# Pacing the gathers of a four-layer graph network in GpSimd's queue, and letting the tails run four stages in three slots

## The chip, the cores and the metric

The kernel runs on one core of a Trainium2 chip. The metric is the time of one execution on the device in microseconds (us). A core has five engines that work side by side, each through its own queue and in order: TensorE (PE, with its weight loads as PEld), VectorE (DVE), ScalarE (ACT), GpSimd (POOL) and SyncE (SP). [...]

## The reference, cut to what matters

Eight feature matrices of 2048 nodes by 128 numbers go through four layers on one sparse graph (each of the 2048 x 2048 entries of `adj` is set with probability 1/128, so a node has some 16 neighbours). Layers 0 and 1 are graph attention transformers:

```
scores = einsum('bnhd,bmhd->bhnm', Q, K) / sqrt(16); masked by adj; softmax
x = layer_norm(h + attn_out @ Wo + bo)
x = layer_norm(x + relu(x @ W1 + b1) @ W2 + b2)
```

Layers 2 and 3 are GAT layers:

```
h = x @ W;  e = leaky_relu(s_i + s_j), masked by adj;  att = softmax(e)
x = layer_norm(einsum('bij,bjd->bid', att, h) + x)
```

A node needs the rows of its neighbours only. A layer can't start on a node before the last layer has finished all of that node's neighbours.

## The kernel before, in words

**Tiles and lists.** The nodes are sorted by degree and cut into 16 tiles of 128, one node per partition. `CAPS` gives the list length of each tile, 30 for the first down to 11 for the last, 277 neighbour slots in all. At the start the kernel counts, sorts and lists (about 180 us).

**Tables and gathers.** Each layer l has a table in DRAM with one row per node: for all eight matrices keys and values together (2048 numbers, layers 0 and 1) or the projected features and two factors (1040 numbers, layers 2 and 3). For one slot of a tile's list, `gather` (L320) is one indirect DMA issued by GpSimd: 128 rows, one per partition, into one of six `kv` buffers. There are 1108 gathers.

**Chunks.** A layer's work is cut into chunks: two slots of one tile in the attention layers, four in the GAT layers. `every` is the list of all chunks in order. An attention chunk runs DVE at L606 (keys times query), L609 (sums over a head) and L620 (weights times values), ACT at L615 (exponentials) and PE at L630 (adds the slots up in PSUM). A GAT chunk runs small DVE steps at L745 to L751, then L757 (weights times features for six of the matrices) beside L762 on ACT (the other two matrices, two scalings per slot), then L766 on DVE (adds half of the slots to the other half) and L772 on PE.

**Tails.** When a tile's last chunk is done, L455 to L462 and L643 or L649 make its normalised output `o`, and two tails, one per half of the eight matrices, carry it on: transposes (L329), products, norms and the projection for the next layer. A tail is a Python generator. It is cut by `yield` into stages, and each stage issues a few instructions. A norm (`normed`) squares on ACT (L471), raises to the power -0.5 on GpSimd (`rs`, L476, "the power" below; 192 of them) and, two yields later, scales on ACT (L480). When both halves are done, GpSimd scatters the tile's rows into the next layer's table (`put_rows`, L494) and `put[l + 1]` goes up by one. In layer 3 each half is multiplied by the gain (L807), offset (L808) and scattered to the output by GpSimd (L810). The tile `n` that a norm writes has two buffers.

**The order.** The order on each engine is that of the Python code. The loop in `layers` goes over the chunks; `now[0]` is the chunk in turn, `now[1]` the first one not yet fetched. In each pass it calls `fetch` once at the top, and three times `slot`, with the parts of chunks between:

```
def slot():
    advance(threads)
    advance(tails)
    fetch()
```

`advance` runs every generator in its list by one stage. `fetch` issues all gathers of as many chunks as it may: at most three chunks (four in the GAT layers) beyond the one in turn, and only once the table holds what a chunk needs. A GAT layer, and layer 1, begins with seven or more early chunks of tiles 0 and 1 whose lists are sorted so that they need only the first 13, 14 or 15 tiles (`EARLY`, `ORDER`); everything else needs all 16. While the next chunk can't be fetched, the loop runs slots alone.

So at the turn into a GAT layer the last tails of the layer before and the early chunks of the new layer are interleaved in the queues of PE and ACT by the slots.

Of the kernel before, what the change touches and what calls it, by code (L numbers as in the profile page):

```python
# [19 lines left out]
NT = N // P  # L20
# [9 lines left out]
CHUNK = 4 * NB * (D + 2)  # L30
# [6 lines left out]
BASE, MANY, FOLD = 28, 16, 2  # L37
# [45 lines left out]
def sparse_path(ctx: ExitStack, tc: tile.TileContext, ins: dict, out: bass.AP, flag: bass.AP):  # L83
# [60 lines left out]
    def buffer():  # L144
        turn[0] += 1
        return bufs[turn[0] % KVB]
# [4 lines left out]
    lists = const.tile([P, sum(CAPS)], I32, name="lists")  # L151
    lmask = const.tile([P, sum(CAPS)], F32, name="lmask")
    first = [sum(CAPS[:t]) for t in range(NT)]

    sorted_lists = const.tile([P, BASE + CAPS[1]], I32, name="sorted_lists")
# [146 lines left out]
    def width(l):  # L302
        return NB * (2 * D if l < 2 else D + 2)
# [15 lines left out]
    def gather(l, index, dst):  # L319
        nc.gpsimd.indirect_dma_start(  # L320
            out=dst, out_offset=None, in_=tables[l][:, :],
            in_offset=bass.IndirectOffsetOnAxis(ap=index, axis=0),
            bounds_check=N - (l < 2), oob_is_err=False,
        )
# [137 lines left out]
        nc.vector.reciprocal(sums, sums)  # L462
        return sums

    def normed(z, dst):

        yield

        ss = small.tile([P, 4], F32, tag="ss", name="ss", bufs=3)
        for i in range(4):  # L470
            nc.scalar.activation(  # L471
                dst[:, i, :], z[:, i, :], AF.Square, bias=eps, scale=D**-0.5,
                accum_out=ss[:, i : i + 1],
            )
        rs = small.tile([P, 4], F32, tag="rs", name="rs", bufs=3)
        nc.gpsimd.tensor_tensor(rs, ss, half, op=ALU.pow)  # L476
        yield
        yield
        for i in range(4):
            nc.scalar.mul(dst[:, i, :], z[:, i, :], rs[:, i : i + 1])  # L480
        yield
# [154 lines left out]
    def sums(l, t, box):  # L636
        box["r"] = reciprocal_sums(l, t, box["w"], NB * (NH if l < 2 else 1), box.get("folded"))
# [353 lines left out]
    def verdict():  # L991
        ok = small.tile([P, 5], F32, tag="ok", name="ok", bufs=1)
        every = score.rearrange("p a t b -> p (a t b)")
        nc.vector.tensor_reduce(ok[:, 3:4], every, axis=AX.X, op=ALU.max)
        nc.vector.tensor_reduce(ok[:, 4:5], every, axis=AX.X, op=ALU.min)
        nc.vector.tensor_single_scalar(ok[:, 3:4], ok[:, 3:4], SCORE_MAX, op=ALU.is_le)
        nc.vector.tensor_single_scalar(ok[:, 4:5], ok[:, 4:5], -SCORE_MAX, op=ALU.is_ge)
        nc.vector.tensor_mul(ok[:, 3:4], ok[:, 3:4], ok[:, 4:5])
        nc.vector.tensor_reduce(ok[:, 0:1], dmin.rearrange("p a b -> p (a b)"), axis=AX.X, op=ALU.min)
        nc.vector.tensor_reduce(ok[:, 1:2], dmax.rearrange("p a b -> p (a b)"), axis=AX.X, op=ALU.max)  # L1000
        nc.vector.tensor_reduce(ok[:, 2:3], over.rearrange("p a b -> p (a b)"), axis=AX.X, op=ALU.max)
        nc.vector.tensor_single_scalar(ok[:, 0:1], ok[:, 0:1], SUM_MIN, op=ALU.is_ge)
        nc.vector.tensor_single_scalar(ok[:, 1:2], ok[:, 1:2], SUM_MAX, op=ALU.is_le)
        nc.vector.tensor_single_scalar(ok[:, 2:3], ok[:, 2:3], 0.0, op=ALU.is_le)
        nc.vector.tensor_mul(ok[:, 0:1], ok[:, 0:1], ok[:, 1:2])
        nc.vector.tensor_mul(ok[:, 0:1], ok[:, 0:1], ok[:, 2:3])
        nc.vector.tensor_mul(ok[:, 0:1], ok[:, 0:1], ok[:, 3:4])
        pk = misc()
        nc.tensor.matmul(pk[:1, :1], ok[:, 0:1], onesc, start=True, stop=True)
        bad = small.tile([1, 1], I32, tag="bad", name="bad", bufs=1)  # L1010
        nc.vector.tensor_scalar(bad, pk[:1, :1], -1.0, float(P), op0=ALU.mult, op1=ALU.add)
        nc.sync.dma_start(flag, bad)
# [3 lines left out]
    tails = []  # L1016

    put = [NT, 0, 0, 0]
    every = []
    blocks = [[{} for _ in range(NT)] for _ in range(4)]  # L1020
    for l in range(4):
        per = 2 if l < 2 else 4
        for t, k, ns, folded in pieces(l, per):
            c = dict(l=l, t=t, k=k, ns=ns, folded=folded, box=blocks[l][t])
            c["last"] = not folded and k + ns == (CAPS[t] if t > 0 else BASE)
            c["run"] = (attention_chunk if l < 2 else gat_chunk)(l, c)
            every.append(c)
    now = [0, 0]

    def advance(group):  # L1030
        for g in list(group):
            if next(g, 0) == 0:
                group.remove(g)

    def fetch():

        while now[1] < len(every):
            c = every[now[1]]
            l, t, k, ns = c["l"], c["t"], c["k"], c["ns"]

            if now[1] - now[0] > (4 if now[1] >= KVB and every[now[1] - KVB]["l"] > 1 else 3):
                return
            resorted = l > 0 and t < 2 and not c["folded"]
            need = NT - max([b for end, b in EARLY[t] if k + ns <= end] + [0] if resorted else [0])
            if put[l] < need:
                return
            c["buf"] = buffer()[:, : ns * width(l)].rearrange("p (s c) -> p s c", s=ns)
            for i in range(ns):
                at = t * BASE if resorted else first[t]
                index = (sorted_lists if resorted else lists)[:, at + k + i : at + k + i + 1]  # L1050
                gather(l, index, c["buf"][:, i])
            now[1] += 1

    def slot():
        advance(threads)
        advance(tails)
        fetch()

    def drain():
        while threads or tails:  # L1060
            advance(threads)
            advance(tails)

    def later(n, make):
        for _ in range(n):
            yield
        yield from make()

    def tail(l, t, box):
        for _ in range(2 if l < 2 else 3):  # L1070
            yield
        outputs(l, t, box)
        part = attention_tail if l < 2 else gat_tail
        tails.append(later(1, lambda: part(l, t, box, 0)))
        tails.append(later(4, lambda: part(l, t, box, 4)))
        yield

    def state(l, t):
        if t >= NT:
            l, t = l + 1, t - NT  # L1080
        if l == 0:
            threads.append(fetch_state(t, blocks[l][t]))
        elif l < 4:
            blocks[l][t].update(x=load_state(t), ready=True)

    def begin(c):
        if c["l"] < 2:
            threads.append(attention_begin(c["l"], c["t"], c["box"]))

    def chunk(i):  # L1090
        return every[i] if 0 <= i < len(every) else dict(l=None, k=None, last=False, folded=False)

    def go(c, times=1):

        for _ in range(times if c["l"] is not None else 0):
            next(c["run"], None)

    def layers():
        threads.append(find_lists(0))
        state(0, 0)  # L1100
        drain()
        fetch()
        begin(every[0])
        drain()
        threads.append(find_lists(1))
        for i in range(len(every) + 2):
            now[0] = i
            fetch()
            c2, c1, c, n1, n2 = (chunk(i + j) for j in range(-2, 3))
            if c["k"] == 0:  # L1110
                l, t = c["l"], c["t"]
                if l == 0:
                    if t + 2 < NT:
                        threads.append(find_lists(t + 2))
                    if t == 0:
                        state(0, 1)
                        threads.append(later(12, lambda: state(0, 2) or iter(())))
                        threads.append(later(12, clear_late))
                    if t in (2, 6):
                        threads.append(order_lists(t // 4))  # L1120
                while l < 2 and "asked" not in c["box"]:
                    slot()
            while i < len(every) and now[1] <= i:
                slot()
            if n2["k"] == 0:
                begin(n2)

            if c2["l"] in (0, 1):  # L1130
                go(c2)
                if c2["last"]:
                    threads.append(tail(c2["l"], c2["t"], c2["box"]))
            if n1["l"] in (2, 3) and n1["folded"]:
                go(n1)
            if c1["l"] in (2, 3) and c1["last"]:
                sums(c1["l"], c1["t"], c1["box"])
            go(c)
            slot()
            go(c)  # L1140
            slot()
            if c1["l"] in (0, 1) and c1["last"]:
                sums(c1["l"], c1["t"], c1["box"])
            go(c1, 2)
            if c1["l"] in (2, 3) and c1["last"]:
                threads.append(tail(c1["l"], c1["t"], c1["box"]))
            slot()
        verdict()
        drain()

    with tc.manual_schedule():
        start()
        layers()
# [525 lines left out]
```

## Time and profile before

| what | value |
|---|---|
| time, median of 4 runs | 3420.86 us (3419.24 to 3422.98) |
| profiled execution, its own time | 3414.06 us |
| its span | 3412.3 us |
| busy: PE, DVE, ACT, POOL | 2747.1, 3062.8, 1427.3, 2216.7 us |
| gathers L320 from `lists` / `sorted_lists` | 955 at 1479 ns, 153 at 1313 ns |
| powers L476 | 192 at 1558 ns |
| DMA | 986.52 MB, mean 289 GB/s |

The page cuts the span into 40 slices of 85 us. Layer 0 begins at about 180 us, layer 1 at about 1200, layer 2 at about 2230 and layer 3 at about 2790. In a row of waits the columns are: engine, line waited at, what ended the wait, total us, times, longest us. In a timeline the columns are: start, duration, engine, line, operation, operands, count, and in brackets the idle time before it with what ended it. Idle time "issue" is time in which the engine waited for nothing that the profile shows.

### The profile page before, as it was taken

Reading aid. Unit: us, or ns where it says so; the run is one execution under the profiler, and the core shown is the slowest. Engines: PE = TensorE matmul, PEld = TensorE weight load, DVE = VectorE, ACT = ScalarE, POOL = GpSimd, SP = SyncE. Lnnn points to the kernel's source line nnn. Section 1 sums busy time; section 2 is a strip of 40 time slices with the busy share of each in tenths; the row PEclk is TensorE's granted clock in tenths of the full one; section 3 lists DMA queues with packets and bytes.
Section 4 is the critical chain, followed back from the end, with each engine's and each line's share of the span. In section 5 each row is a group of like instructions: output and inputs, shape, how many; then the busy total and the mean of one; then the engine's idle time right before and its main releaser. Section 6 shows DMA issues by size and latency. Waiting matters only on the chain.

```text
span 3412.3 us, 34694 instructions
## 1 busy us (share of the span) xinstructions
PE 2747.1 (81%) x10618; PEld 1585.8 (46%) x10618; DVE 3062.8 (90%) x2727; ACT 1427.3 (42%) x4972; POOL 2216.7 (65%) x1501
## 2 busy tenths in 40 slices
PE   5657888888989997788888989985888985667775
PEld 4423455545555553455545555652445543223332
DVE  7789999999999999999999999975888875788886
ACT  5711333334444442233333444443655653444444
POOL 0056788688657654465676766646788765688874
PEclk9878989989999999899999999988999997889888
DMA  8587787888888777687887887757999986889883
GB/s 332 190 319 276 292 293 278 312 298 289 307 316 297 290 264 292 226 328 292 307 321 293 299 307 291 274 196 258 338 340 348 345 308 237 282 296 318 297 291 129
DMA packets 200881, 986.52 MB, mean 289 GB/s; under 512 B 32174, under 2 KB 33968, under 8 KB 128692
## 3 DMA queue, kind: packets, MB, share of 16 engines
q0 software_dynamic: 175280, 890.45, 72.0%
q1 hardware_dynamic: 20502, 75.52, 5.9%
q10 hardware_dynamic: 4904, 18.24, 1.4%
q8 instruction: 87, 1.43, 0.2%
q14 instruction: 108, 0.88, 0.1%
HBM read 937.16 MB, written 91.55 MB: 301 GB/s over the span
## 4 chain that ended last, share of the span: by engine, by line
DVE 33%; PE 24%; issue 18%; DMA 10%; POOL 6%; ACT 3%; POOLq 0%; DVEq 0%; ACTq 0%
DVE kv L620 11%; DVE kv L606 11%; PE acc L630 8%; PE acc L772 6%; DMA kv<-table,lists 5%; POOL kv L320 5%; DMA kv<-table,sorted_lists 2%; DVE sc L609 2%; DVE kv L757 2%; DVE kv L766 2%; PE m L712 2%; PE m L691 1%; PE m L329 1%; POOL rs L476 1%; DVE sums L455 1%
## 5 line engine op out<-in xcount | busy, mean ns | idle before, releaser
L320 POOL DMA_INDIRECT kv<-table,lists x955 | 1412.0, 1479 | 359.1 <-issue 210.6
L630 PE MATMUL acc<-kv,ident 128*128 128x512 f32 x2200 | 1112.3, 636 | 223.8 <-DVE kv L620 223.3
L772 PE MATMUL acc<-kv,ident 128*128 128x512 f32 x1184 | 613.4, 667 | 203.3 <-DVE kv L766 156.4
L630 PEld LDWEIGHTS acc<-kv,ident 128*128 128x128 f32 x2200 | 414.7, 202 | 659.8 <-issue 371.2
L606 DVE TENSOR_TENSOR kv<-kv,q 128x2048 f32<-128x2048 f32 (+1 forms) x282 | 629.2, 2231 | 19.1 <-DMA kv<-table,lists 10.0
L609 DVE TENSOR_REDUCE sc<-kv 128x128 f32<-128x2048 f32 (+1 forms) x284 | 634.0, 2232 | 9.2
L620 DVE TENSOR_TENSOR kv<-kv,w 128x2048 f32<-128x2048 f32 (+1 forms) x284 | 631.4, 2223 | 5.8 <-ACT w L615 5.8
L476 POOL TENSOR_TENSOR rs<-ss,half 128x4 f32<-128x4 f32 x192 | 299.1, 1558 | 413.1 <-ACT n L471 411.4
L471 ACT ACTIVATE n<-m,eps 128x128 f32<-128x128 f32 x768 | 271.3, 366 | 567.8 <-PE m L712 215.7
L772 PEld LDWEIGHTS acc<-kv,ident 128*128 128x128 f32 x1184 | 241.4, 214 | 505.8 <-issue 296.6
L757 DVE TENSOR_TENSOR kv<-kv,pair 128x3072 f32<-128x3072 f32 (+1 forms) x150 | 466.2, 3108 | 1.0
L766 DVE TENSOR_TENSOR kv<-kv 128x2048 f32<-128x2048 f32 (+1 forms) x150 | 296.1, 1974 | 143.1 <-ACT kv L762 143.1
L762 ACT ACTIVATE kv<-kv,ws 128x128 f32<-128x128 f32 x1108 | 339.2, 405 | 146.9 <-DVE ws L751 119.7
L480 ACT ACTIVATE n<-m,rs 128x128 f32<-128x128 f32 x768 | 218.9, 369 | 364.8 <-POOL rs L476 364.3
L615 ACT ACTIVATE w<-sc,lmask 128x64 f32<-128x64 f32 x554 | 164.9, 351 | 457.5 <-DVE sc L609 457.2
L320 POOL DMA_INDIRECT kv<-table,sorted_lists x153 | 200.8, 1313 | 113.9 <-PE acc L630 43.7
L329 PE MATMUL m<-ident,n 128*128 128x128 f32 x640 | 106.2, 287 | 81.5 <-ACT n L480 81.4
L494 POOL DMA_INDIRECT table<-rows,perm x57 | 101.1, 1774 | 106.8 <-ACT rows L518 27.7
L471 ACT ACTIVATION_READ_ACCUMULATOR n<-m,eps 128x1 f32 x768 | 157.3, 205 | 0.0
L712 PE MATMUL m<-w_L_w,hT 128*128 128x128 f32 x1024 | 156.2, 275 | 0.0
L329 PEld LDWEIGHTS m<-ident,n 128*128 128x128 f32 x640 | 81.1, 145 | 138.0 <-ACT n L480 87.2
L712 PEld LDWEIGHTS m<-w_L_w,hT 128*128 128x128 f32 x1024 | 134.9, 192 | 0.0
(234 smaller groups left out, 3252.7 us busy)
## 6 DMA issues: line engine op xcount, KB each, us to landing
kept<-xT SPq DMA_DIRECT2D x48, 512.0 KB, 7.1
xT<-kept SPq DMA_DIRECT2D x48, 512.0 KB, 6.7
kv<-in_adj_dram SPq DMA_DIRECT2D x16, 1024.0 KB, 6.3
table<-kv ACTq DMA_DIRECT2D x16, 1024.0 KB, 4.9
kv<-table,lists POOLq DMA_INDIRECT x955, 7.1
kv<-in_x_nodes_dram SPq DMA_DIRECT2D x16, 512.0 KB, 6.9
kv<-table,sorted_lists POOLq DMA_INDIRECT x153, 6.4
found<-cand POOLq DMA_DIRECT2D x16, 64.0 KB, 3.3
```

The source lines that it names most:

```text
L320: nc.gpsimd.indirect_dma_start(out=dst, out_offset=None, in_=tables[l][:, :], in_offset=bass.IndirectOffsetOnAxis(ap=index, axis=0), bound ...
L471: nc.scalar.activation(dst[:, i, :], z[:, i, :], AF.Square, bias=eps, scale=D**-0.5, accum_out=ss[:, i : i + 1],)
L476: nc.gpsimd.tensor_tensor(rs, ss, half, op=ALU.pow)
L606: nc.vector.tensor_mul(kk, kk, q[:, None].to_broadcast([P, ns, NB, D]))
L609: nc.vector.tensor_reduce(sc[:, :ns].rearrange("p s (b h) -> p (s b) h", h=NH), kk.rearrange("p s b (h j) -> p (s b) h j", h=NH), axis=AX. ...
L620: nc.vector.tensor_mul(vv, vv, w[:, k : k + ns, :].rearrange("p s (b h) -> p (s b) h", h=NH)[:, :, None, :] .to_broadcast([P, ns * NB, HD, ...
L630: nc.tensor.matmul(acc[:, j, :], merge if c["folded"] else ident, kv[:, i, 4 * j : 4 * j + 4, D:], start=k + i == 0, stop=c["last"] and i ...
L712: nc.tensor.matmul(y[:, j, :], hT[:, f, j, :], wt["2"][:, f, :], start=False, stop=f == 1, skip_group_check=True,)
L757: nc.vector.tensor_mul(hv[:, :, :nv, :], hv[:, :, :nv, :], wc[:, :, :nv, None].to_broadcast([P, ns, nv, D]))
L762: nc.scalar.mul(hv[:, i, b, :], hv[:, i, b, :], ws[:, i, b - nv : b - nv + 1])
L766: nc.vector.tensor_add(hv[:, : ns - left], hv[:, : ns - left], hv[:, left:ns])
L772: nc.tensor.matmul(acc[:, j, :], merge if c["folded"] else ident, hv[:, i, 4 * j : 4 * j + 4, :], start=k + i == 0, stop=c["last"] and i = ...
```

## The change

`fetch` issues gathers one at a time and remembers in `now[2]` how far a chunk has come. If the chunk after the one in turn is already fetched, one call issues at most one gather (layers 0 and 1) or two (layers 2 and 3); else as many as it may, as before. The call at the top of a pass is made only if the next chunk isn't fetched yet. Within a slot `fetch` comes after the tails' stages, so what the tails issue on GpSimd in that slot stands ahead of the slot's gathers.

`hurry` holds while the chunk in turn is of the last tile of layer 2, or of a GAT layer whose table is not full yet. Then the tails advance once more in every third slot. `normed` gets a parameter for its two yields, which no caller sets.

```diff
-    def normed(z, dst):
+    def normed(z, dst, wait=2):
...
-        yield
-        yield
+        for _ in range(wait):
+            yield
...
-    now = [0, 0]
+    now = [0, 0, 0]
+    beat = [0]
...
     def fetch():
 
-        while now[1] < len(every):
+        for _ in range((1 if every[min(now[1], len(every) - 1)]["l"] < 2 else 2)
+                       if now[1] > now[0] + 1 else 2 * CHUNK):
+            if now[1] == len(every):
+                return
             c = every[now[1]]
...
-            c["buf"] = buffer()[:, : ns * width(l)].rearrange("p (s c) -> p s c", s=ns)
-            for i in range(ns):
-                at = t * BASE if resorted else first[t]
-                index = (sorted_lists if resorted else lists)[:, at + k + i : at + k + i + 1]
-                gather(l, index, c["buf"][:, i])
-            now[1] += 1
+            i = now[2]
+            if i == 0:
+                c["buf"] = buffer()[:, : ns * width(l)].rearrange("p (s c) -> p s c", s=ns)
+            at = t * BASE if resorted else first[t]
+            index = (sorted_lists if resorted else lists)[:, at + k + i : at + k + i + 1]
+            gather(l, index, c["buf"][:, i])
+            now[1:] = (now[1] + 1, 0) if i + 1 == ns else (now[1], i + 1)
+
+    def hurry():
+
+        c = every[min(now[0], len(every) - 1)]
+        return c["l"] == 2 and c["t"] == NT - 1 or c["l"] > 1 and put[c["l"]] < NT
 
     def slot():
         advance(threads)
         advance(tails)
         fetch()
+        beat[0] += 1
+        if beat[0] % 3 == 0 and hurry():
+            advance(tails)
...
             now[0] = i
-            fetch()
+            if now[1] <= i + 1:
+                fetch()
```

## The prediction

> **What bounds the kernel now.** I read the page first, then busy time by stage, then who waits for whom, then the timeline.
>
> ```profile
> DVE  7789999999999999999999999975888875788886
> POOL 0056788688657654465676766646788765688874
> DMA  8587787888888777687887887757999986889883
> ```
>
> DVE's row is nines through the attention layers (slices 3 to 26) and drops where the GAT layers begin. The same by stage (columns: busy us of PE, PE's loads, DVE, ACT, POOL, then PE clock, DMA share, GB/s):
>
> ```profile
> 200.00:2230.00 2030.00, 1761.20 (x7206) 1041.60 (x7207) 1995.04 (x1191) 751.69 (x2611) 1350.71 (x787) 0.94 0.80 294
> 2230.00:2340.00 110.00, 74.87 (x335) 46.26 (x334) 54.89 (x53) 49.55 (x184) 49.08 (x44) 0.83 0.53 188
> 2340.00:2780.00 440.00, 369.45 (x1397) 207.17 (x1395) 375.61 (x401) 239.00 (x943) 348.74 (x281) 0.94 0.94 340
> 2780.00:2880.00 100.00, 64.76 (x260) 38.61 (x261) 55.63 (x54) 46.00 (x183) 51.57 (x44) 0.81 0.65 228
> 2880.00:3345.00 465.00, 325.29 (x792) 145.96 (x791) 392.67 (x436) 205.67 (x777) 365.09 (x287) 0.87 0.88 300
> ```
>
> Attention: DVE 1995 of 2030 us. The two turns into a GAT layer: DVE half idle. Inside the GAT layers POOL is the full one, although the page says 65%: its instructions follow each other with a fixed gap of about 0.30 us. Gaps counted up to 0.31 us each, from the timeline, POOL is taken for 349 + 77 = 426 of 440 us in layer 2 and 365 + 80 = 445 of 465 in layer 3. What DVE waits for from 2230 on:
>
> ```profile
> DVE kv L766 <- ACT kv L762: 143.1, 52, 9.5
> DVE kv L745 <- DMA kv<-table,lists: 45.9, 2, 33.3
> DVE kv L745 <- DMA kv<-table,sorted_lists: 27.5, 9, 10.6
> ```
>
> L762 is late because ACT stands at L480 for the power (`ACT n L480 <- POOL rs L476`, 364 us in all). One such wait:
>
> ```profile
> 2284.58 0.99 POOL L320 DMA_INDIRECT kv<-table,sorted_lists  x1 [0.30 <-issue]
> 2285.87 0.99 POOL L320 DMA_INDIRECT kv<-table,sorted_lists  x1 [0.30 <-issue]
> 2286.89 1.05 POOL L476 TENSOR_TENSOR rs<-ss,half 128x4 f32<-128x4 f32 x1
> 2287.97 1.14 ACT L480 ACTIVATE n<-m,rs 128x128 f32<-128x128 f32 x4 [7.71 <-POOL rs L476]
> ```
>
> The squares ended at 2277.5; the power ran at 2286.9, behind eight gathers.
>
> **What the Trainium skill says.** "Perfetto Trace Analysis", What "DMA-bound" means: an issuing engine whose track is solid DMA slices is itself the limit; the trace agrees, as above. Same page, DMA Instruction — SWDGE: the slice is descriptor generation, not movement; here 1.0 to 3 us against 7.1 us to landing. "SBUF — State Buffer", Who interferes with whom: a DVE instruction with two SBUF inputs blocks a GpSimd one that reads SBUF; of 80 GAT gathers longer than 1.8 us, 76 begin while L766 (two SBUF inputs) runs. "DMA: Bandwidth & Descriptors", Two DMAs through the same engine are not ordered: a dependent DMA waits for the semaphore; after each L494 the next gather stands 3 to 5 us.
>
> **The change, part by part.** No instruction is added or removed: 1108 gathers, 192 powers, 57 scatters into tables in both. `wait=2` is the old pair of yields: nothing. By the order of the instructions in each queue, DVE's and SP's are the same in both programs, PE's and ACT's differ at the two turns alone, and POOL's differs all through.
>
> *Powers among gathers, layers 2 and 3.* 55 powers now stand after two gathers of a chunk, not after all. A power is 2 x (1.03 + 0.30) = 2.7 us earlier in the queue, and DVE's usual 5.6 us stop at L766 once per tile could shrink to 3. But the same 4.2 us-plus of gathers per chunk still pass through POOL, which has only 14 us of other idle time in layer 2 and 20 in layer 3. DVE gains until L745 waits for gathers in place of L766 for the power. Layer 2: **-4** (0 to -14).
>
> *Outputs, layer 3.* L810 goes out in the slot before the chunk's gathers, four gathers (5 us) earlier. The next tile's squares wait for that store, since `n` has two buffers: 57 us of ACT waits, longest 10.7. With POOL's two gathers between L810 and the next power, the idle 5.9 + 1.7 + 5.6 us at 2949 to 2970 mostly goes: -10; elsewhere -3. **-13** (0 to -20, POOL's spare time).
>
> *Turn 1 to 2* (2230 to 2340). The last table scatter is at 2318.5; DVE stands 33.3 us for the gather behind it. In the new order the second half's first power of tile 15 is ahead of the eight gathers: -9. `hurry` takes four tail stages per three slots, so one chunk's eight scales (2.4 us) and eight matmuls (3.6) fewer are ahead of the tail: -6. Against it, the gathers of the fifth early chunk (2250 to 2257 before) stand behind the first half's power, whose squares end at 2271: DVE gets that chunk at about 2279, +5. **-10** (+3 to -18).
>
> *Turn 2 to 3* (2780 to 2880). Scatters at 2809.2, 2833.1, 2859.4. Each waits for the landing of gathers of the same table, and gathers then for it. The first now has 12 gathers ahead of it, not 16; the fourth chunk moves behind it. Down the new queue, with 1.3 us a gather or power, some 6.5 us from the last gather to landing and 4 us after a scatter: the first gathers start at 2775.7 as before, the twelfth is out at about 2792.5 and landed at 2799, scatter one; from 2803 eight gathers and two powers, out at 2816, landed at 2823, scatter two; from 2827 eight gathers and the last tile's powers, out at 2840; then its scaling, transpose and copies, 8 us as before (2849.8 to 2858.9 with a chunk's scales between): scatter three at 2848. **-11** (0 to -18). What follows a turn is POOL-full and starts earlier, so it isn't lost later.
>
> *Attention layers.* Here one gather per slot stands behind the slot's power, where the pair stood before it. The queue order shows each power moved ahead of one pair. POOL has room (1351 + 0.3 x 787 = 1587 of 2030), but powers wait on ACT's squares (up to 11 us), and now a pair needed three chunks later waits too. Who waits for the pair: L606, and DVE has no slack. I set each power's end, plus the gathers behind it (1.75 + 0.30 us each), plus 8.0 us to landing (median in layer 1), against the start of the L606 that reads the pair. Median slack is about 2 us where it was 10, and 13 pairs are late by 17 us together; with 7.0 us landing 10 pairs by 6; with 9 us 43 pairs by 52. Landing may quicken when pairs are spread. I take **+12** (0 to +40).
>
> Queued behind a waiting power in the GAT layers are now the chunk's other two gathers; DVE waits for them four chunks later. The squares are ready before POOL comes (5.7 us of `rs <- n` waits in layer 2, 21.5 in layer 3, of which 11.5 are at the two stores above), and four gathers still lie between a tile's two powers: no cost.
>
> Sum: -4 - 13 - 10 - 11 + 12 = **-26 us**. The profiled execution was 3414.1 us (span 3412.3 and 1.8 around it), which gives 3388; the median of the runs is 6.8 us above it, so 3395.
>
> **Rivals.**
> (A) *Slower: attention pairs late.* DVE's 98% means that each late pair is paid in full. For: slack falls from 10 to 2 us, and the sum is steep in landing time. Against: DVE now waits 16.6 us for gathers in all attention, and a stall leaves later pairs slack. It decides from the point where the sum passes the 38 us of gains: landing of about 8.7 us behind a power. At 9 us: 52 - 38 = +14, 3435.
> (B) *Hidden anyway.* The turns are set by the serial scatter, landing, gather rounds and the fifth chunk's delay eats the rest: GAT gains fall to 12, attention costs 12: 3421.
> (C) *POOL isn't full.* If the 0.30 us gaps are slack, each of some 28 tiles gains 2.7 us: -76, with the turns -21, outputs -13 and attention +12: 3323. Against: the gaps stay in bursts with nothing to wait for (2324 to 2334).
> That the change does nothing is excluded: half of POOL's queue order moves.
>
> **How the numbers follow.** Mine 0.52, A 0.20, B 0.22, C 0.06. About 0.2% (7 us) is what can be told from no change. Mine is faster in nearly all of its width (3368 to 3412): 0.51, with C 0.06 and 0.09 of B: 0.66. B leaves 0.09 same and 0.04 slower, and mine 0.01; A gives 0.03 same and 0.17 slower: same 0.12, slower 0.22. The range 3362 to 3436 takes in A at 9 us landing and leaves C out.
>
> **What would show it.** Right: L480's waits on L476 fall well under 364 us; the waits for `table` at the turns shrink, the 33.3 us one to about 23; POOL stays full in layers 2 and 3; L606 begins to wait for `kv<-table,lists`, some 10 to 15 us. Wrong: L606 waits of 40 us or more (A); last scatters of the turns as late as before relative to the last attention chunk (B); POOL's gaps shrinking and layer 2 over 20 us shorter (C).

## The result, and the profile after

The kernel after takes 3426.06 us (median of 34 runs, 3415.10 to 3435.64), the kernel before 3420.85 (55 runs). The ratio is 1.0012, 95% interval 1.0007 to 1.0018: some 4 us slower, where 26 us less were forecast.

The profiled execution of after took 3436.41 us (span 3434.6), 10 above its median. That of before was 7 below its own. So the two traces lie 22 us apart and the medians 5: stages are read from the traces below, totals from the ratios.

The page of the kernel after, the same three rows of slices:

```profile
DVE  7779999999999988999999999985888875888896
POOL 0056788688667655465677666755788875788884
DMA  8586877887787767587788878766999996899884
```

A dip to 88 has come into DVE's row in slices 15 and 16, at 1200 to 1370 us, the turn from layer 0 to 1. Busy time by stage in after, the bounds shifted with the stages (columns: busy us of PE, PE's loads, DVE, ACT, POOL, then PE clock, DMA share, GB/s):

```profile
203.00:2266.00 2063.00, 1762.37 (x7202) 1036.72 (x7203) 1995.88 (x1190) 751.22 (x2609) 1389.00 (x785) 0.94 0.78 289
2266.00:2372.00 106.00, 73.81 (x338) 46.43 (x337) 55.69 (x54) 49.75 (x187) 54.18 (x48) 0.87 0.63 216
2372.00:2811.00 439.00, 370.49 (x1397) 207.56 (x1396) 376.07 (x401) 239.19 (x944) 353.00 (x281) 0.94 0.94 339
2811.00:2914.00 103.00, 77.01 (x260) 45.11 (x261) 55.98 (x56) 45.87 (x183) 55.02 (x45) 0.78 0.67 228
2914.00:3366.00 452.00, 318.46 (x790) 143.88 (x789) 392.31 (x433) 205.39 (x777) 367.22 (x284) 0.89 0.90 305
```

DVE's work in the attention layers is the same 1996 us, but it takes 2063 us of time and not 2030. Layer 3 (last row) is 13 us shorter, layer 2 and the turns are nearly what they were. Some waits of DVE in after (line waited at, what ended it, total us, times, longest):

```profile
DVE kv L766 <- ACT kv L762: 139.8, 54, 8.4
DVE kv L745 <- DMA kv<-table,lists: 33.4, 4, 24.1
DVE kv L606 <- DMA kv<-table,lists: 27.5, 12, 9.6
DVE kv L606 <- DMA kv<-table,sorted_lists: 24.3, 5, 9.3
```

The attention layers' L606 now waits 51.8 us for gathers; in before it was 16.6. In both some 10 us of it is the very first gather of layer 0. The 33.3 us wait at the turn into layer 2 is 24.1.

The table that carries the rest shows when DVE starts a given chunk: us later than in before (negative: earlier), from the profiled execution of each kernel. Each experiment is described further down.

| DVE starts | before at | after | e1 | e2 | e5 | e6 | e8 | e9 |
|---|---|---|---|---|---|---|---|---|
| layer 0, first L606 | 190.0 | 3.3 | -1.3 | -1.0 | -0.5 | -1.4 | -2.0 | -2.3 |
| layer 0, 129th L606 | 1125.5 | 9.7 | -0.9 | 7.2 | 6.1 | -2.3 | -3.6 | -1.4 |
| layer 0, last (142nd) L606 | 1218.1 | 16.3 | -1.1 | 6.8 | 5.6 | -2.5 | -3.8 | -1.6 |
| layer 1, 165th L606 | 1389.9 | 30.8 | -2.3 | 19.8 | 9.8 | 10.9 | -4.0 | -2.8 |
| last L606 | 2229.4 | 36.8 | -2.9 | 27.0 | 15.8 | 11.4 | -4.3 | -3.3 |
| layer 2, 11th L757 | 2351.7 | 31.6 | -6.6 | 28.9 | 12.7 | 7.7 | -7.2 | -1.5 |
| layer 2, 71st L757 | 2753.4 | 30.8 | -8.1 | 30.3 | 10.9 | 6.3 | -8.3 | 0.6 |
| layer 3, 85th L757 | 2886.3 | 33.7 | -7.0 | 28.5 | 11.9 | 4.9 | -12.0 | 1.3 |
| layer 3, 97th L757 | 2982.5 | 26.1 | -16.4 | 30.3 | 2.1 | -4.0 | -21.5 | -9.8 |
| last L757 | 3368.9 | 21.2 | -21.2 | 31.3 | -2.7 | -8.8 | -26.4 | -15.0 |

In the column "after" the attention layers lose 33.5 us (3.3 to 36.8). The turn from layer 0 to 1 (142nd to 165th L606) makes 14.5 of it, and 13.0 in e2, whose attention part is the same. The 6.6 us just before (129th to 142nd) are this one execution's: e2 and e5, with the same program there, show nothing of the kind. Layer 3 gains 12.5.

**What happens at that turn.** Four rows of before's GpSimd timeline are enough (start, duration, then the line, in brackets the idle time and what ended it):

```profile
1211.52 3.02 POOL L476 TENSOR_TENSOR rs<-ss,half 128x4 f32<-128x4 f32 x1 [8.65 <-ACT n L471]
1214.75 1.05 POOL L494 DMA_INDIRECT table<-rows,perm  x1 [0.21 <-issue]
1220.22 1.02 POOL L320 DMA_INDIRECT kv<-table,sorted_lists  x1 [4.42 <-PE m L329]
1221.55 2.07 POOL L320 DMA_INDIRECT kv<-table,sorted_lists  x1 [0.31 <-issue]
```

The table scatter L494 follows the power at once, and the next pair follows the scatter. The same place in after:

```profile
1227.80 3.01 POOL L476 TENSOR_TENSOR rs<-ss,half 128x4 f32<-128x4 f32 x1 [9.17 <-ACT n L471]
1231.01 1.06 POOL L320 DMA_INDIRECT kv<-table,sorted_lists  x1 [0.20 <-issue]
1232.37 2.93 POOL L320 DMA_INDIRECT kv<-table,sorted_lists  x1 [0.30 <-issue]
1240.83 2.50 POOL L494 DMA_INDIRECT table<-rows,perm  x1 [5.53 <-DMA kv<-table,sorted_lists]
1243.36 1.05 POOL L476 TENSOR_TENSOR rs<-ss,half 128x4 f32<-128x4 f32 x1
1247.75 1.06 POOL L320 DMA_INDIRECT kv<-table,sorted_lists  x1 [3.35 <-PE m L691]
```

The pair that was moved behind the power stands between the power and the scatter. The power waits 9.2 us for ACT, and the pair with it. The scatter writes the table that the pair reads, so it waits 5.5 us until the pair has landed. The next pair starts 4.4 us after the scatter's end, as it did in before; the view names PE for this wait, but at other scatters of the turns it names the scatter's landing (`table<-rows,perm`). From power to next gather it is 20 us, where it was 9. DVE, which needs that next pair:

```profile
1257.00 2.29 DVE L606 TENSOR_TENSOR kv<-kv,q 128x2048 f32<-128x2048 f32 x1 [7.17 <-DMA kv<-table,sorted_lists]
```

At the next two scatters L606 waits 6.5 us (at 1306) and 9.3 us (at 1356). In before it waited there too, 1.2 and 5.4 us, since gathers of the same table stood ahead of these scatters already; so not all of it is new.

### The profile page after: what moved, and what is told of

It is laid out like the page before. It is cut to its first block, busy times and chain, and to the rows that moved or that the text cites. A ratio compares the mean times of both kernels' runs of the same rounds, so it can differ in the third digit from the quotient of the medians.

```text
span 3434.6 us, 34691 instructions
## 1 busy us (share of the span) xinstructions
PE 2757.2 (80%) x10618; PEld 1588.2 (46%) x10618; DVE 3064.9 (89%) x2727; ACT 1426.8 (42%) x4972; POOL 2273.1 (66%) x1501
## 5 line engine op out<-in xcount | busy, mean ns | idle before, releaser
L320 POOL DMA_INDIRECT kv<-table,lists x955 | 1428.8, 1496 | 316.2 <-issue 218.4
L606 DVE TENSOR_TENSOR kv<-kv,q 128x2048 f32<-128x2048 f32 (+1 forms) x282 | 629.3, 2232 | 56.5 <-DMA kv<-table,lists 27.5
L609 DVE TENSOR_REDUCE sc<-kv 128x128 f32<-128x2048 f32 (+1 forms) x284 | 634.0, 2232 | 9.2
L620 DVE TENSOR_TENSOR kv<-kv,w 128x2048 f32<-128x2048 f32 (+1 forms) x284 | 631.3, 2223 | 0.8 <-ACT w L615 0.8
L476 POOL TENSOR_TENSOR rs<-ss,half 128x4 f32<-128x4 f32 x192 | 329.8, 1718 | 425.6 <-ACT n L471 423.8
L757 DVE TENSOR_TENSOR kv<-kv,pair 128x3072 f32<-128x3072 f32 (+1 forms) x150 | 466.2, 3108 | 0.9
L766 DVE TENSOR_TENSOR kv<-kv 128x2048 f32<-128x2048 f32 (+1 forms) x150 | 296.2, 1974 | 139.8 <-ACT kv L762 139.8
L480 ACT ACTIVATE n<-m,rs 128x128 f32<-128x128 f32 x768 | 219.6, 370 | 396.9 <-POOL rs L476 396.6
L320 POOL DMA_INDIRECT kv<-table,sorted_lists x153 | 211.3, 1381 | 106.8 <-PE acc L630 36.7
L494 POOL DMA_INDIRECT table<-rows,perm x57 | 98.8, 1733 | 107.5 <-ACT rows L545 26.8
L691 PE MATMUL m<-n1T,w_L_gnn_W 128*128 128x512 f32 x256 | 132.8, 602 | 3.1 <-ACT n L480 2.7
```

What stands on the lines that cost most here:

```text
L320: nc.gpsimd.indirect_dma_start(out=dst, out_offset=None, in_=tables[l][:, :], in_offset=bass.IndirectOffsetOnAxis(ap=index, axis=0), bound ...
L606: nc.vector.tensor_mul(kk, kk, q[:, None].to_broadcast([P, ns, NB, D]))
L609: nc.vector.tensor_reduce(sc[:, :ns].rearrange("p s (b h) -> p (s b) h", h=NH), kk.rearrange("p s b (h j) -> p (s b) h j", h=NH), axis=AX. ...
L620: nc.vector.tensor_mul(vv, vv, w[:, k : k + ns, :].rearrange("p s (b h) -> p (s b) h", h=NH)[:, :, None, :] .to_broadcast([P, ns * NB, HD, ...
L757: nc.vector.tensor_mul(hv[:, :, :nv, :], hv[:, :, :nv, :], wc[:, :, :nv, None].to_broadcast([P, ns, nv, D]))
L766: nc.vector.tensor_add(hv[:, : ns - left], hv[:, : ns - left], hv[:, left:ns])
```

## The experiments

Eleven kernels ran, in three groups, each beside the kernel before on the same chip; before's medians there were 3418.39, 3420.80 and 3420.61 us. The group is told with each.

To change one part at a time, `fetch` asks a function `pace(c)` for the rule of a chunk: `None` fetches whole chunks, also at the top of a pass, as in before; 1 or 2 is the number of gathers per slot, as in after.

### e1: attention layers as before (group 1)

```diff
+    def pace(c):
+        l, t = c["l"], c["t"]
+        return None if l < 2 else 2
...
-        for _ in range((1 if every[min(now[1], len(every) - 1)]["l"] < 2 else 2)
-                       if now[1] > now[0] + 1 else 2 * CHUNK):
+        loose = pace(every[min(now[1], len(every) - 1)]) is None
+        free = loose or now[1] <= now[0] + 1
+        for _ in range(2 * CHUNK if free else pace(every[min(now[1], len(every) - 1)])):
```

> Layers 0 and 1 fetch whole chunks as in the kernel before; layers 2 and 3 and the fourth tail stage are as in the kernel after. Theory T (the loss is made in the attention layers, where a pair of gathers now stands behind a power; the GAT layers gain): layer 3 keeps its 13 us, the turns about nothing, so 3421 - 15 = about 3406 us, and DVE's waits at L606 fall back to those of before (about 17 us). Rival R1 (the attention pairs cost nothing lasting, the loss of 5 us comes from the GAT layers or the turns): as the kernel after, 3426. Rival R2 (a shift in the attention layers is given back at the next turn): 3421 or more.

Measured: 3394.47 us, ratio to before 0.9924 (0.9910 to 0.9938), so 26 us faster than before, and 12 us below what theory T gave. The GAT part of the change does gain, and R1 and R2 fall.

### e2: the attention layers' pacing alone (group 1)

```diff
-        return None if l < 2 else 2
+        return 1 if l < 2 else None
...
-        return c["l"] == 2 and c["t"] == NT - 1 or c["l"] > 1 and put[c["l"]] < NT
+        return False
```

> Only layers 0 and 1 are paced, one gather per slot; layers 2 and 3 fetch whole chunks and no tail stage is added. Theory T: the kernel before plus 20 us (15 to 30), so about 3441, with L606 waiting for gathers about 50 us. Rival R1: 3421. Rival R2: 3421 with L606 waiting all the same.

Measured: 3449.51 us, ratio 1.0090 (1.0075 to 1.0106): 31 us slower than before, at the upper edge of what theory T gave. Its DVE waits at L606:

```profile
DVE kv L606 <- DMA kv<-table,lists: 23.5, 8, 10.2
DVE kv L606 <- DMA kv<-table,sorted_lists: 21.9, 4, 8.8
```

That is 45.4 us, 28.8 more than in before, and column e2 loses 28.0 in the attention layers: DVE pays the late pairs in full, and nothing is given back (the column stays at 27 to 31 to the end). The two parts add up: 31 - 26 = 5, and after is 4 us slower than before.

### e3 and e4: the fourth tail stage alone, and GAT pacing without it (group 1)

e3 has `pace` return `None` everywhere and keeps `hurry`; e4 has the `pace` of e1 and a `hurry` that is always false.

> Only the fourth tail stage in three slots at the two turns into GAT layers; every layer fetches whole chunks. Theory T: the turns into layers 2 and 3 are 0 to 6 us shorter each and nothing else moves, so 3410 to 3421. Rival R3 (the tails' stages are not what holds the turns; more of them early put copies and scales ahead of the early chunks): 3421 to 3430.

> Only layers 2 and 3 are paced, two gathers per slot; no fourth tail stage. Theory T: layer 3 gains 13 us and layer 2 about 1; the turn into layer 2 loses up to 10 because the second early chunk is split round the table scatter: 3405 to 3417. Rival R3 says that the gain at the turns needs this part and not the fourth stage, so that this kernel equals the first one (attention as before) within 3 us; theory T has it 3 to 10 us slower than the first.

Measured: e3 3421.15 us, ratio 1.0008 (1.0000 to 1.0015), so nothing or up to 5 us lost, on the border between T and R3; e4 3398.17 us, ratio 0.9935 (0.9921 to 0.9949), so 22 us gained, 7 us below T's band. The pacing carries most of the gain. e4 is 4 us above e1, where T has 3 to 10 and R3 at most 3; the two intervals overlap, so this doesn't tell T from R3.

### e5: whole chunks at the turn from layer 0 to 1 (group 2)

```diff
-        return None if l < 2 else 2
+        return (None if l == 1 and put[1] < NT else 1) if l < 2 else 2
```

> The kernel after, but layer 1's early chunks are fetched whole while layer 1's table is not full: at the turn from layer 0 to 1 no pair stands between a power and the table scatter. Theory T1 (that turn makes 13 to 21 of the attention layers' loss: a pair behind a power delays the scatter that waits for the pair to land, and then the gathers behind the scatter): 3426 less 13 to 21, so 3405 to 3413. Rival R4 (the loss is made of single late pairs all over layers 0 and 1): 3420 or more.

Measured: 3407.52 us, ratio 0.9958 (0.9943 to 0.9974): 18 us faster than after by the two ratios (4 + 14). In the turn (1205 to 1355 us) L606's waits are back at those of before (6.6 us, twice):

```profile
DVE kv L606 <- DMA kv<-table,sorted_lists: 5.8, 2, 4.5
```

So the pair between power and scatter does cost, as theory T1 has it, and R4 is out as the whole cause. In its trace the turn loses 4.2 us (5.6 to 9.8), not 14.5. What R4 names exists too: outside the turn column e5 still rises by 6.1 in layer 0 and 6.0 in layer 1, and e5 stays some 12 us above e1.

### e6: one gather of each pair ahead of the power (group 2)

```diff
     def slot():
+        attention = every[min(now[1], len(every) - 1)]["l"] < 2
+        if attention:
+            fetch()
         advance(threads)
         advance(tails)
-        fetch()
+        if not attention:
+            fetch()
```

The diff is to after.

> The kernel after, but in layers 0 and 1 a slot's gather is issued ahead of the tails' stages of that slot, so that of each pair one gather stands ahead of the power and one behind. Theory T1 (the place behind a power that waits for ACT is what costs): a part of the loss goes, since the pair ends one gather (2 us) earlier, though its second half still waits for the power: 3410 to 3420. Rival R5 (one gather per slot instead of a pair at the top of a pass is what costs): 3426 as the kernel after.

Measured: 3404.91 us, ratio 0.9951 (0.9936 to 0.9967): 21 us better than after, more than T1 gave. One gather per slot is not what costs, so R5 falls. Column e6 shows where it gained: layers 0 and 1 outside the turn are as in before (-1.1 and +0.5), while the turn still loses 13.4. Single pairs are late by 1 or 2 us at most places, and one gather (2 us) earlier is enough. At the scatter it isn't, since one gather of the pair still stands between power and scatter.

Not every late pair stands behind a power. The longest wait of layer 0 outside the turn comes in after, e2 and e5 alike (4.7, 5.3 and 4.8 us). In after:

```profile
827.01 3.06 POOL L494 DMA_INDIRECT table<-rows,perm  x1 [0.30 <-DVE o L643]
831.71 2.81 POOL L335 DMA_INDIRECT xs<-in_x_nodes_dram,perm  x1 [0.31 <-issue]
845.09 2.29 DVE L606 TENSOR_TENSOR kv<-kv,q 128x2048 f32<-128x2048 f32 x1 [4.68 <-DMA kv<-table,lists]
```

The pair that this L606 reads is issued at 834.82 and 837.07, behind a table scatter and two indirect DMAs of the threads, generators that order the lists and fetch the input rows (L405 at 830.37 and L335), with no power near. In before it stood ahead of L405 and L335. In e6, where a gather goes ahead of threads and tails, the wait is 1.9 us (at 833).

Thus e5 and e6 split the loss between them: 13 us (the traces of e2 and e6) to 18 us (e5's ratio) at the turn, 12 us (e5 less e1) to 18 us (31 less 13) in single late pairs.

### e7: each GAT power issued twice (group 2)

In e1 a second power follows at once, with the same inputs, into a tile that nobody reads (64 of them).

```diff
         nc.gpsimd.tensor_tensor(rs, ss, half, op=ALU.pow)
+        if more:
+            spare2 = small.tile([P, 4], F32, tag="spare2", name="spare2", bufs=3)
+            nc.gpsimd.tensor_tensor(spare2, ss, half, op=ALU.pow)
```

> Attention as before, GAT layers paced (3394 in the first call), and each of the 64 powers of layers 2 and 3 is issued twice, the second into a tile that nobody reads. Theory T (GpSimd is full in layers 2 and 3 though the page shows 65 to 81% busy): each extra power costs 1.03 + 0.30 us where GpSimd is full, some 50 of the 64, so +67 us, 3455 to 3470. Rival C (the 0.30 us gaps and the waits are slack): +0 to +15, 3394 to 3410.

Measured: 3454.33 us, 60 us more than e1. The group of the added powers, from e7's groups of GpSimd (busy us, mean ns, idle time before them):

```profile
L479 POOL TENSOR_TENSOR spare<-ss,half 128x4 f32<-128x4 f32 x64 | 65.0, 1015 | 0.0
```

They took 65 us and the kernel became 60 us longer, just under theory T's band. The extra power is behind the real one, so its own norm doesn't wait for it; what stands behind it in the queue does. Set against e1's trace, DVE falls behind by 27 us in layer 2, 7 at the turn into layer 3 and 27 in layer 3. GpSimd is full in layers 2 and 3, and rival C falls. (The expectation counted a gap of 0.30 us with each; there is none.)

### e8: the fourth tail stage at the first GAT turn only (group 2)

```diff
-        return c["l"] == 2 and c["t"] == NT - 1 or c["l"] > 1 and put[c["l"]] < NT
+        return c["l"] == 2 and put[2] < NT
```

The diff is to e1.

> Attention as before, GAT layers paced, the fourth tail stage only at the turn into layer 2 and not at the one into layer 3. From the profiles of the first call that stage saved 8 us at the turn into layer 2 and cost 5 at the turn into layer 3: then this is 5 us faster than with both, 3389. Rival R3 (the stage does at both turns what it does in the medians, 4 us together): 3394 to 3398.

Measured: 3389.78 us, ratio 0.9908 (0.9893 to 0.9923), about 5 us below e1 as expected, though the two intervals overlap. The last three table scatters of the turn into layer 3 in e1, with the stage:

```profile
2798.49 1.01 POOL L494 DMA_INDIRECT table<-rows,perm  x1 [7.92 <-issue]
2822.38 1.01 POOL L494 DMA_INDIRECT table<-rows,perm  x1 [6.50 <-ACT rows L545]
2852.18 2.36 POOL L494 DMA_INDIRECT table<-rows,perm  x1 [11.06 <-ACT score L547]
```

and in e8, without it:

```profile
2803.04 1.01 POOL L494 DMA_INDIRECT table<-rows,perm  x1 [6.65 <-DMA kv<-table,sorted_lists]
2824.88 1.05 POOL L494 DMA_INDIRECT table<-rows,perm  x1 [0.21 <-issue]
2849.36 1.01 POOL L494 DMA_INDIRECT table<-rows,perm  x1 [7.81 <-DMA kv<-table,sorted_lists]
```

The stage brings the first scatter forward by 4.6 us. But the last half's power then stands behind eight gathers after the second scatter, not four (2840.1 in e1, 2835.3 in e8), and in e1 the last scatter waits 11.1 us for that tail on ACT, where in e8 it waits for gathers to land. The turn ends on the last scatter. In the traces e8 is 4.8 us better here (-8.3 to -12.0, e1 -8.1 to -7.0).

### e9 and e10: a third buffer for `n` (group 3)

```diff
-        n2 = work.tile([P, 4, D], F32, tag="n", name="n2")
+        n2 = work.tile([P, 4, D], F32, tag="n", name="n2", bufs=3)
```

This stands at all three places where such a tile is made: in the kernel before (e9) and in e8 (e10).

> The kernel before with three buffers in place of two for the tile n that a norm writes. In layer 3 the squares then no longer wait for the output store of the tile before (66 us of ACT waits in 12 places in the kernel before). Theory T (layer 3's 13 us come from that wait, which the earlier store L810 shortens): most of the 13 us come in this way too, 3408 to 3414. Rival R6 (they come from the powers' new place between the gathers): 3418 to 3421.

> Attention as before, GAT layers paced, the fourth tail stage at the turn into layer 2 only (3390 in the last call), and three buffers for n. Theory T: the store's wait has been shortened from 66 to 37 us already, so a third buffer adds little, 3384 to 3390. Rival R6: if the store counts for nothing, 3390.

Measured: e9 3395.13 us, ratio 0.9924 (0.9911 to 0.9938), 13 us below theory T's band; e10 3382.62 us, ratio 0.9886 (0.9870 to 0.9902), 1 us below its band. ACT's waits from 2880 to 3400 us, in before:

```profile
ACT n L480 <- POOL rs L476: 105.5, 31, 11.5
ACT n L471 <- DMA out_dram<-n,perm: 66.0, 12, 10.7
```

in e8, where most L810 go out three or four gathers earlier:

```profile
ACT n L480 <- POOL rs L476: 129.3, 32, 11.5
ACT n L471 <- DMA out_dram<-n,perm: 37.0, 9, 6.0
```

and in e9, where the wait for the store is gone altogether:

```profile
ACT n L480 <- POOL rs L476: 142.9, 32, 11.6
```

Column e9 gains 16.3 us from the 85th L757 to the last and nothing before that; the rest of the 26 is within what one profiled execution differs from the median (7 us for before). So the squares' wait for the output store costs layer 3 some 16 us. What leaves that wait comes back in part at L480. e10 adds the third buffer to the pacing and is the fastest kernel here, 39 us below before. The two gains don't add up (26 by the buffer, 31 by e8): with the buffer in place the pacing gains only 2.6 us more in layer 3 (18.9 from the 85th L757 to the last in e10's trace, 16.3 in e9's). So what the pacing gains in layer 3 is mostly this wait, and R6 falls as the main cause.

### e11: whole early chunks at the turn into layer 2 (group 3)

```diff
-        return None if l < 2 else 2
+        return None if l < 2 or l == 2 and put[2] < NT else 2
```

The diff is to e8.

> As the 3390 kernel, but the early chunks of layer 2 are fetched whole, as before, until layer 2's table is full. Its first chunk of gathers is then no longer split round the table scatter, which made DVE start that chunk 11 us later. Theory T (the turn ends with the last scatter's chain, so the late first chunk costs nothing and the pacing brings 2 to 4 us there by letting powers pass): 3392 to 3396. Rival R7 (the split costs at the turn): 3380 to 3386.

Measured: 3391.36 us, ratio 0.9917 (0.9903 to 0.9930), within 3 us of e8, with intervals that overlap, and just under theory T's band; R7's gain is not seen. DVE's first GAT chunk is on time again, and the turn as a whole takes the same time within the spread.

## Why the prediction was wrong, point by point

**Attention, forecast +12, measured +31: the step that failed.** This term was mis-sized in both its parts.

*Single late pairs.* The prediction's table gave 17 us for all late pairs, the turn included, and 12 was taken; outside the turn alone 12 to 18 were measured. The 8.0 us from issue to landing was not the mistake: in the 15 places of after where L606 waited over 0.2 us for a gather (the first of layer 0 left out), that gather landed 8.1 us after its issue began, in the median (7.4 to 11.7). Nor did landing quicken, as was thought possible: the median over the gathers from `lists` between 1400 and 2230 us went from 8.0 to 8.7. But the table held pairs against powers only. Behind the stages of a slot a pair stands behind whatever these issue on GpSimd, table scatters and the threads' DMAs too (the 4.68 us wait above). How much of the 12 to 18 us each of the two makes was not tried.

*The turn from layer 0 to 1*: 13 to 18 measured. The table set each pair against its own power. It left out that the scatter behind the power waits for this very pair, and that the following pair waits for the scatter. The prediction followed just that chain (gathers, landing, scatter, gathers) at the turn into layer 3, and cites the Trainium skill for it, "DMA: Bandwidth & Descriptors", Two DMAs through the same engine are not ordered; at the turn into layer 1 it wasn't applied. (The 3 to 5 us that it gives after each L494 hold at the turns, but for one of 6.9; elsewhere in before the next gather mostly starts 0.3 us after the scatter.)

Rival A, attention pairs late, is what happened, by this chain and by the pairs' place in the queue rather than by a landing of 9 us. Rival B's 3421 lies nearest to the result by luck: it sets a gain of 12 against a loss of 12, where the runs show 26 and 31.

**Turn into layer 2, forecast -10, in the trace of after -5 (36.8 to 31.6).** DVE's longest wait fell as forecast, 33.3 to 24.1. But another one came, at the first GAT chunk, since here too the first pair of gathers now stands between a power and a scatter. Both in after's timeline:

```profile
2282.26 0.19 DVE L745 TENSOR_TENSOR kv<-kv,own 128x32 f32<-128x32 f32 x1 [11.39 <-DMA kv<-table,sorted_lists]
2364.45 0.17 DVE L745 TENSOR_TENSOR kv<-kv,mine 128x16 f32<-128x16 f32 x1 [24.14 <-DMA kv<-table,lists]
```

Set against the end of layer 1, the last scatter moved by 4 us, not 10 (2351.4 - 36.8 = 2314.6, before 2318.5). The term of 9 us for the second half's power was too large: that power is 1.7 us earlier. Both powers of tile 15 stand behind the second scatter, which is 2.6 us later than before because it waits for landings:

```profile
2311.95 1.01 POOL L494 DMA_INDIRECT table<-rows,perm  x1 [7.22 <-DMA kv<-table,sorted_lists]
```

e11 shows that the split first chunk is not what kept the gain small. Which other place for the second scatter would free the 10 us was not tried.

**Turn into layer 3, forecast -11, in the trace of after +3.** Set against layer 2's end the scatters came at 2805.6, 2831.3 and 2862.4, not at 2799, 2823 and 2848. In e1, where the same queue order can be followed undelayed, the first gather started 2 us later than taken, two instructions beside L766 lasted 1.6 and 1.9 us longer, and the scatter came 7.9 us after the last gather, not 6.5: 7 us together. The last tail took 12.1 us from its power to the scatter, where 8 were taken. And the fourth tail stage itself costs about 5 us here, by e8's trace and median. `hurry` was given a gain and no price.

**Layer 2, forecast -4**: about -1 (-0.8 in after, -1.5 in e1). DVE's waits at L766, which were to shrink, went from 143.1 to 139.8 us. Of the 55 powers 35 moved ahead of two gathers and 20 of only one. **Layer 3, forecast -13**: -12.5 in after, -14.2 in e1, and mostly by the mechanism named, as e9 and e10 show. **GpSimd full**: right, by e7 and by after's windows (353 + 0.30 x 281 = 437 of 439 us in layer 2, a little too much, since a power has no gap ahead of it). **L480's waits** were to fall well under 364 us and rose:

```profile
ACT n L480 <- POOL rs L476: 396.6, 140, 11.6
```

From stage to stage they are 88 before and 109 after in the attention layers, 169 and 158 in layer 2 with both turns, 107 and 130 in layer 3. In the GAT layers, where GpSimd is full, the delay moved from one place to another and did not shrink (276 and 288).

By the measured parts: GAT -26 where -38 was forecast, attention +31 where +12 was.

## What to carry to other kernels

When an instruction is moved behind a waiting one, follow what stands behind it in turn, and look at everything that now stands ahead of it, not only at the instruction that it was moved for. A scatter that must wait for a moved gather to land hands the delay on to the gathers behind the scatter: 20 us from power to next gather here, where it was 9. Where one part of a change works on an engine that is full and another on a layer where a different engine has no slack, price and try them apart: here half of the change gains 26 us and the other half loses 31. A wait that a reordering shortens can be a missing buffer: a third `n` took all of it away and, put into the kernel before by itself, gained as much as the whole GAT part of the change (26 us each).

## What the runs showed of the hardware

A power whose squares are ready starts on GpSimd without a gap, after another power (64 times, idle 0.0) as after a gather (2772.06 to 2772.08 in e1). A gather starts 0.30 us after a gather and some 0.20 us after a power. So the gap goes with the gather: a power among gathers costs about 1.0 us (1.05 + 0.20 - 0.30; e7: 60 us for 64), where the prediction counted 1.33.

How long GpSimd takes to issue a gather depends on what DVE runs when the issue begins. Counted in before: of the gathers that begin during L606 and L620 (200 to 2230 us) 261 of 273 took over 1.8 us, during L609 none of 212; in the GAT layers (2340 to 3345 us) 74 of 91 during L766, and none of 249 during L757, which runs longer. L606, L620 and L766 read two operands from SBUF, L609 reads one, and L757 takes its second, `pair`, from PSUM. During any other instruction of DVE the median is 1.0 to 1.4 us. This is a count and no experiment: no run here changed an operand's place.
